# First-batch scores from h^T and S h^T in a two-layer graph kernel: score path, weight loads and epilogue order changed

## The chip, the cores and the metric

The kernel runs on one core of a Trainium2 chip. The metric is the device time of one execution in microseconds (us). The core has a matrix engine (TensorE, PE in the profile; its weight loads are listed apart as PEld), a vector engine (VectorE, DVE), a scalar engine (ScalarE, ACT), a general engine (GpSimd, POOL) and a queue engine for transfers (SyncE, SP). Each engine works through its own instructions in the order in which the program lists them for it; between engines, semaphores carry "this is ready".

## The reference, cut to what matters

There are 16 batches of 1024 nodes with 128 features and a symmetric 0/1 adjacency per batch. Layer 0 is a gated attention layer, layer 1 a tanh attention with four heads; both are followed by a residual and a layer norm.

```python
h = x @ Ww.T + Wb
e = (h @ A) @ h.T
e = e + e.T                      # = h S h^T with S = A + A^T
scores = where(adj > 0, e, 0.0)
attention = softmax(scores, axis=1) * adj
h_prime = relu(attention @ h)
ic, fc, oc = sigmoid(h_prime @ wi_u + x @ wi_x), ...
x = layernorm(x + oc * tanh(ic * h_prime + fc * x))
# layer 1, per head: h1 = X conv_w + conv_b
hh = relu(tanh(adj * (h1 attn_w h1^T)) @ h1)
x = layernorm(x + relu(relu(mean over heads) + x))
```

The scores of layer 0 are softmaxed down a column, and e is symmetric, so the kernel treats a row of blocks as the column that it needs.

## The kernel before, in words

A batch's 1024 nodes are eight blocks of 128. In layer 0, `score(j)` (line 343) multiplies block j against the blocks from j on and writes them to `R`; `turn_score(j)` (line 359) turns the blocks beyond the diagonal and writes them to the rows still to come, by PE transposes and ACT copies in the first batch (b = 0), and through DRAM in the others. `find_edges` (line 391) makes a 0/1 mask of the adjacency; `mask(j)` (line 401) multiplies row j by it on DVE while taking the row's maximum, and ACT takes the exponential with its sum. `weigh(j)` (line 414) divides h by that sum (`hz`), multiplies the row by the adjacency on DVE, and starts `back(j - 1)` (line 431), which adds the previous row's share of the output on PE.

Scores come from a fused form: e_jk = x_j (W^T S W) x_k^T + a part that depends on j alone + a part that depends on k alone. `q_w` is W^T S W, `c_col` is added as the q projection's bias (`project_q`, line 306), and the part by row, r, is made as one more column of `multiply_h` (line 323); `add_h` (line 333) adds it a bias. The eviction of a score (line 353) adds r from column G - 1 of `h`, so it waits for `h`. The first rows of h have to be made before the first score leaves PSUM.

The chain of the fused weights is written at lines 142 to 166: A and Ww are loaded and turned, then S W, q_w, c_col and S b. Six idle matmuls (`keep_at_work`) stand ahead of it and one in its midst. `join_weights` (line 168) is a generator in three parts for layer 1: a difference of convolution weights, its transposes, its product with the attention weights, and another product `ms`; each part ends with an ACT copy of 128x512.

`load_late_weights` (line 99) issues the late loads on SP: three gate columns, a convolution bias, `cw_last` to partitions 1 to 127, `cw_in` in two parts, `aw`, and `wu_b`. On SP's queue they stand behind the first batch's eight adjacency loads, `x` and the second batch's xT, and ahead of the second's adjacency.

The order of the work at the start is written out by hand, as names of pieces that `run` (line 577) calls: W xT, L adjacency, X x, Q the q projection, H and h the product and sum for h, S scores, T turns, A mask with exponential, E edges, B weigh, R ReLU, P rows of h', G gates, I inner gate with tanh, O outer gate, V and N the layer norm. `first` and `second` are batches 0 and 1; the second's pieces stand among the first's to give PE work. After that, `layer1_step` (line 613) runs over 16 batches, four heads and eight blocks, with the coming batches' pieces in tables (`BETWEEN`, `AHEAD`, `FIRST`). Small PSUM tiles share four buffers (`small`, line 61), so a fifth waits for the first's eviction.

The end of the first batch's layer 0 is a chain: the ReLU (line 440), `rows_hp` (line 446), `gates` and `forget` (line 483), `inner` (line 519), `outer` (line 531) and `turn_first_x1` (line 588), which makes x1^T for layer 1; `head_uT` and `rows` then start layer 1.

Of the kernel before, what the change touches and what calls it, by code (L numbers as in the profile page):

```python
# [19 lines left out]
P = 128  # L20
# [4 lines left out]
def two_layer_adjacency_kernel(  # L25
# [19 lines left out]
    nc = tc.nc  # L45
# [15 lines left out]
    def small(name):  # L61
        return ps_sc.tile([P, 512], F32, tag="sc", name=name)
# [7 lines left out]
    nc.gpsimd.memset(mhalf, -0.5)  # L70

    a_in = sb.tile([P, P], F32, tag="hz", name="a_in", bufs=4)
    nc.scalar.dma_start(a_in, A)
    ww_in = sb.tile([P, P], F32, tag="hz", name="ww_in", bufs=4)
    nc.sync.dma_start(ww_in, Ww)
    wb_col = consts.tile([P, 1], F32, name="wb_col")
    nc.scalar.dma_start(wb_col, Wb.rearrange("(d o) -> d o", o=1))
    rows_x = sb.tile([3, P], F32, tag="s1", name="rows_x", bufs=4)
# [18 lines left out]
    wu_b = consts.tile([P, 3, D], F32, name="wu_b")  # L97

    def load_late_weights():
        for g, w in enumerate((wi_u, wf_u, wo_u)):  # L100
            nc.sync.dma_start(gate_u[:, g : g + 1], w.rearrange("(d o) -> d o", o=1))
        nc.sync.dma_start(cw_in[0:1], conv_b.rearrange("(o h) d -> o h d", o=1))
        nc.sync.dma_start(cw_last[1:P], conv_w[:, D - 1, :].partition_broadcast(P - 1))
        for f0, f1 in ((0, 112), (112, D - 1)):
            nc.sync.dma_start(
                cw_in[1 + f0 : 1 + f1], conv_w[:, f0:f1, :].rearrange("h f d -> f h d")
            )
        nc.sync.dma_start(aw, attn_w.rearrange("h i j -> i h j"))
        for g, w in enumerate((wi_u, wf_u, wo_u)):
            nc.sync.dma_start(wu_b[:, g, :], w.partition_broadcast(P))  # L110


# [5 lines left out]
    nc.gpsimd.memset(cw_last[0:1], 0.0)  # L118
# [23 lines left out]
    pa, pw, ps, pc = small("p_a"), small("p_ww"), small("p_s"), small("p_c")  # L142
    nc.tensor.transpose(pa[:, :P], a_in, ident)
    nc.vector.tensor_add(a_sym, pa[:, :P], a_in)
    nc.tensor.matmul(pw[:, :P], ww_in, ident, start=True, stop=True)
    nc.scalar.copy(wwT, pw[:, :P])
    nc.gpsimd.tensor_copy(b_wide, wb_col.to_broadcast([P, P]))
    nc.tensor.matmul(ps[:, :P], a_sym, ww_in, start=True, stop=True)
    nc.vector.tensor_copy(s_ww, ps[:, :P])
    keep_at_work(1)  # L150
    pq, px = small("p_q"), small("p_x")
    nc.tensor.matmul(pq[:, :P], s_ww, ww_in, start=True, stop=True)
    nc.vector.tensor_copy(q_w, pq[:, :P])
    nc.tensor.matmul(pc[:, 0:1], s_ww, wb_col, start=True, stop=True)
    nc.vector.tensor_copy(c_col, pc[:, 0:1])
    nc.tensor.matmul(pc[:, 1:2], a_sym, wb_col, start=True, stop=True)
    nc.vector.tensor_copy(sb_col, pc[:, 1:2])

    def gates_x():
        nc.tensor.matmul(px[:, :3], rows_x, ident[:3, :3], start=True, stop=True)  # L160
        nc.vector.tensor_copy(gate_x, px[:, :3])

    def finish_weights():
        pt = small("p_bsb")
# [2 lines left out]

    def join_weights():

        nc.vector.tensor_sub(cw, cw_in, cw_last)  # L170
        pt = small("p_cwT")
        for hd in range(H):
            nc.tensor.transpose(pt[:, ts(hd, P)], cw[:, hd, :], ident)
        nc.scalar.copy(cwT.rearrange("p h f -> p (h f)"), pt)
# [4 lines left out]
        nc.scalar.copy(caT.rearrange("p h f -> p (h f)"), pt)  # L179
# [103 lines left out]
    def layer0(b):  # L283
# [22 lines left out]
        def project_q(q):  # L306
            if q == 0:
                t["qT"] = sb.tile([P, N], F32, tag="qT0", name=f"qT0_{b}", bufs=1)
            if (b, q) == (0, 1):
                ps = small("pT_q0_second")  # L310
                nc.tensor.matmul(ps, q_w, t["xT"][:, 512:], start=True, stop=True)
                nc.vector.tensor_scalar_add(t["qT"][:, 512:], ps, c_col)
                return
            if (b, q) != (0, 0):
                return project_T(t["qT"], q_w, t["xT"], c_col, f"q0_{b}", [q])
            ps = small("pT_q0_first")
            nc.tensor.matmul(ps, q_w, t["xT"][:, :512], start=True, stop=True)
            for at, to in ((0, P), (P, 512)):
                nc.scalar.activation(
                    t["qT"][:, at:to], ps[:, at:to], AF.Identity, bias=c_col  # L320
                )

        def multiply_h(g):

# [8 lines left out]
        def add_h(g):  # L333
            h, ks = t["h"], GROUPS[g]
            nc.vector.tensor_add(
                h[:, ks[0] : ks[-1] + 1, :], t["ph", g],
                wb_row.unsqueeze(1).to_broadcast([P, len(ks), G]),
            )
            if g == len(GROUPS) - 1:
                t["gate"] = sb.tile([P, NB, 3], F32, tag="gate", name=f"gate_{b}")  # L340
                nc.vector.tensor_copy(t["gate"], h[:, :, D : D + 3])

        def score(j, halves=None):
            if j == 0:
# [53 lines left out]
            engine.tensor_scalar(m, adj_t[b, j], 0.0, None, ALU.is_gt)  # L398
            t["edge", j] = m.rearrange("p (k d) -> p k d", d=P)

        def mask(j):
            s, nmax = t["R"][:, :, j, :], -3e38
            for ks in (ts(0, BH), ts(1, BH)) if (b, j) == (0, 0) else [slice(NB)]:
                top = sb.tile([P, 1], F32, tag="top", name=f"top_{b}_{j}_{ks.start}", bufs=4)
                nc.vector.tensor_tensor_reduce(  # L405
                    s[:, ks], s[:, ks], t["edge", j][:, ks], 1.0, nmax, ALU.mult, ALU.max, top
                )
                nmax = top
            nmax = sb.tile([P, 1], F32, tag="nmax", name=f"nmax_{b}_{j}", bufs=4)
            nc.vector.tensor_scalar_mul(nmax, top, -1.0)  # L410
            t["z", j] = sb.tile([P, 1], F32, tag="z", name=f"z_{b}_{j}", bufs=4)
            nc.scalar.activation(s, s, AF.Exp, bias=nmax, accum_out=t["z", j])  # L412

        def weigh(j):

# [155 lines left out]
            if j + 1 < NB:  # L571
                pieces[f"T{j}"] = partial(turn_score, j)
        if b == 0:
            del pieces["S1"], pieces["T0"]
        return pieces

    def run(pieces, names):
# [297 lines left out]
```

## Time and profile before

The median is 2413.15 us of 3 runs (2412.75 to 2415.81). The profiled execution took 2412.88 us, with a span of 2410.9 us on the core and a granted TensorE clock of 0.999.

| what | value |
|---|---|
| PE busy | 2399.1 us (100% of the span) |
| DVE busy | 1554.7 us (64%) |
| ACT busy | 1065.3 us (44%) |
| POOL busy | 603.3 us (25%) |
| DMA, mean | 82 GB/s |

Busy time is the time in which an engine has an instruction in work; a PE that is busy is not one at its peak, since matmuls overlap each other. The chain that ended last is followed back from the last instruction, at each step to what released it. A float32 matmul shows as two records with two weight loads; a transpose shows as one.

### The profile page before, as it was taken

The numbers are of one execution on the slowest core, as the hardware profiler recorded it, in microseconds if no ns is written. First come the engines' busy times: TensorE is split into PE (matmuls) and PEld (weight loads), VectorE is DVE, ScalarE is ACT, GpSimd is POOL, SyncE is SP. The second block draws the span as 40 slices with busy tenths as digits, with TensorE's granted clock in tenths as the row PEclk, the third lists the DMA queues.
The fourth block names the chain that finished last, engine by engine and source line by source line (L and its number), as shares of the span: only waits on it lengthen the run. The fifth ranks groups of instructions, "written<-read, shape, count | busy, mean of one in ns | idle before, by whom it ended". The sixth has DMA issues, their size and how long they took to land.

```text
span 2410.9 us, 20160 instructions
## 1 busy us (share of the span) xinstructions
PE 2399.1 (100%) x5981; PEld 1095.2 (45%) x5981; DVE 1554.7 (64%) x3280; ACT 1065.3 (44%) x1500; POOL 603.3 (25%) x373
## 2 busy tenths in 40 slices
PE   8999999999999999999999999999999999999999
PEld 5444444444444444444444444444444444444444
DVE  7666666666667666676666665666666576666555
ACT  6544344443444444445344454434444344443333
POOL 1314131241312413123131231312214132141000
PEclk9999999999999999999999999999999999999999
DMA  5334151341514424243242422425234252341010
GB/s 185 79 75 126 36 139 36 95 115 48 127 44 100 101 52 123 50 108 87 60 115 57 113 75 70 105 61 123 61 72 112 53 127 57 79 114 34 18 27 9
DMA packets 474349, 197.04 MB, mean 82 GB/s; under 512 B 414964, under 2 KB 440303, under 8 KB 474240
## 3 DMA queue, kind: packets, MB, share of 16 engines
q1 hardware_dynamic: 455626, 129.03, 22.9%
q0 software_dynamic: 18320, 66.66, 9.4%
q8 instruction: 48, 0.79, 0.1%
q14 instruction: 61, 0.50, 0.1%
q10 hardware_dynamic: 294, 0.07, 0.0%
HBM read 136.19 MB, written 59.51 MB: 81 GB/s over the span
## 4 chain that ended last, share of the span: by engine, by line
PE 98%; DVE 1%; ACT 0%; issue 0%; POOL 0%; POOLq 0%; DVEq 0%; ACTq 0%
PE sc L630 36%; PE acc L636 36%; PE acc L435 9%; PE sc L350 5%; PE pR L601 5%; PE pT_u L234 5%; PE pR_h L331 1%; PE pT_q L234 1%; DVE R L405 0%; DVE R L427 0%; PE idle L139 0%; DVE st L210 0%; DVE edge L398 0%; DVE u L523 0%; PE pt L454 0%
## 5 line engine op out<-in xcount | busy, mean ns | idle before, releaser
L631 DVE TENSOR_TENSOR s<-sc,adj 128x512 f32<-128x512 f32 x1008 | 685.5, 688 | 711.8 <-PE sc L630 688.3
L632 ACT ACTIVATE s<-s 128x1024 f32<-128x1024 f32 x504 | 533.9, 1059 | 1055.9 <-DVE s L631 896.6
L630 PE MATMUL sc<-uT,x1T 128*128 128x512 f32 x2048 | 962.4, 592 | 0.0
L636 PE MATMUL acc<-s,h 128*128 128x512 f32 x2016 | 947.3, 592 | 0.0
L636 PEld LDWEIGHTS acc<-s,h 128*128 128x128 f32 x2016 | 380.5, 190 | 484.7 <-issue 477.5
L630 PEld LDWEIGHTS sc<-uT,x1T 128*128 128x128 f32 x2048 | 386.9, 190 | 469.3 <-issue 403.5
L398 POOL TENSOR_SCALAR edge<-adj 128x1024 uint8<-128x1024 f32 x120 | 332.8, 2773 | 316.2 <-DVE top_None L405 314.1
L214 POOL TENSOR_TENSOR rs<-rs,mhalf 128x8 f32<-128x8 f32 (+3 forms) x35 | 54.0, 1543 | 884.4 <-DVE rs L213 884.4
L435 PE MATMUL acc<-R,hz 128*128 128x512 f32 x512 | 240.8, 593 | 2.3 <-DVE R L427 1.4
L412 ACT ACTIVATE R<-R,nmax 128x1024 f32<-128x1024 f32 x128 | 147.3, 1151 | 84.9 <-DVE nmax L410 76.0
L405 DVE CUSTOM_DVE_ANT_0 R<-R,edge 128x1024 f32<-128x1024 f32 (+1 forms) x128 | 154.9, 1210 | 0.5 <-PE turn L368 0.5
L427 DVE TENSOR_TENSOR R<-R,adj 128x1024 f32<-128x1024 f32 x129 | 154.6, 1199 | 0.0
L435 PEld LDWEIGHTS acc<-R,hz 128*128 128x128 f32 x512 | 96.6, 190 | 124.7 <-issue 115.0
L350 PE MATMUL sc<-xT,qT 128*128 128x512 f32 (+3 forms) x384 | 145.2, 487 | 0.5 <-ACT R L369 0.3
L353 ACT ACTIVATE R<-sc,h 128x512 f32<-128x512 f32 (+1 forms) x192 | 111.1, 581 | 51.6 <-PE sc L350 44.1
L467 POOL TENSOR_TENSOR x1T<-hp,wu_b 128x1024 f32<-128x1024 f32 x45 | 106.4, 2363 | 103.2 <-DVE hws L473 63.7
L234 PE MATMUL pT_u<-x1T,ms 128*128 128x512 f32 x256 | 120.5, 592 | 0.0
L601 PE MATMUL pR<-cw,x1T 128*128 128x512 f32 x256 | 117.7, 598 | 0.0
L350 PEld LDWEIGHTS sc<-xT,qT 128*128 128x128 f32 x384 | 69.6, 190 | 69.6 <-issue 59.8
L300 POOL DMA_DIRECT2D adj<-in_adjT_dram x112 | 65.7, 587 | 92.6 <-DVE s L631 92.6
L654 DVE SCALAR_TENSOR_TENSOR sum<-acc,sum 128x512 f32<-128x512 f32 x95 | 61.3, 686 | 42.2 <-PE acc L636 42.2
L604 ACT COPY h<-pR 128x512 f32<-128x512 f32 x128 | 72.5, 593 | 27.9 <-PE pR L601 26.1
(144 smaller groups left out, 1129.3 us busy)
## 6 DMA issues: line engine op xcount, KB each, us to landing
adj<-in_adjT_dram POOLq DMA_DIRECT2D x112, 512.0 KB, 4.0
adj<-in_adjT_dram SPq DMA_DIRECT2D x16, 512.0 KB, 8.4
x<-in_x_dram SPq DMA_DIRECT2D x16, 512.0 KB, 5.3
xT<-in_xT_dram SPq DMA_DIRECT2D x15, 512.0 KB, 4.6
dram_hp<-turn_hp SPq DMA_DIRECT2D x15, 512.0 KB, 2.6
hp<-dram_hp SPq DMA_DIRECT2D x60, 128.0 KB, 3.2
dram_x<-turn_x SPq DMA_DIRECT2D x15, 512.0 KB, 2.9
x1T<-dram_x SPq DMA_DIRECT2D x60, 128.0 KB, 5.4
```

Of the source, the lines that this page charges most:

```text
L234: nc.tensor.matmul(ps, w, src[:, ts(q, 512)], start=True, stop=True)
L350: nc.tensor.matmul(ps[:, : at - lo], t["qT"][:, ts(j, P)], t["xT"][:, lo:at], start=True, stop=True)
L398: engine.tensor_scalar(m, adj_t[b, j], 0.0, None, ALU.is_gt)
L405: nc.vector.tensor_tensor_reduce(s[:, ks], s[:, ks], t["edge", j][:, ks], 1.0, nmax, ALU.mult, ALU.max, top)
L412: nc.scalar.activation(s, s, AF.Exp, bias=nmax, accum_out=t["z", j])
L427: nc.vector.tensor_mul(s[:, ks], s[:, ks], adj[:, ks])
L435: nc.tensor.matmul(t["acc"][:, ts(q, 512)], t["hz", j], t["R"][:, ts(q, BH), j, :], start=(j == 0), stop=(j == NB - 1),)
L601: nc.tensor.matmul(ps, x1T_t[b][:, ts(k, P)], cw.rearrange("p h d -> p (h d)"), start=True, stop=True)
L630: nc.tensor.matmul(ps, x1T[:, ts(m, P)], uT[:, ts(q, 512)], start=True, stop=True)
L631: nc.vector.tensor_mul(s[:, ts(q, 512)], ps, adj[:, ts(q, 512)])
L632: nc.scalar.activation(s, s, AF.Tanh)
L636: nc.tensor.matmul(acc[:, ts(q, 512)], h1[:, ts(hd, D)], s[:, ts(q, 512)], start=(m == 0), stop=(m == NB - 1),)
```

## The change

For the first batch the scores are taken from h^T itself. `project_h` makes h^T from Ww^T and xT (pieces K0 and K1; `place_h`, k1, is the second half's eviction), and `project_g` makes S h^T in three parts (g0 to g2 of 128, 384 and 512 columns), evicted on DVE. A score is then a product of S h^T and h^T, and its eviction is a plain copy without the row's number. The pieces Q0 and Q1 of the first batch go; q_w, c_col, S b and the row number are still made, since the other batches use them, but behind the first scores (`weigh_Ww`, `weigh_all`).

Ww is loaded ahead of A, on ACT's queue instead of SP's, and turned first, by a transpose. The first row's mask, its exponential and its score are cut into pieces of their own (A0.0, A0.1, A0.e, S0.0, S0.1). Late weights are loaded ahead of x and of the second batch's xT, and `cw_last` is loaded to all 128 partitions, with row 0 set to zero after that. The subtraction in `join_weights`, and the copy of the gates' columns in `add_h` (in every batch), go from DVE to POOL. The generator of joined weights has one stop more, and its parts stand among the rows of the first batch, instead of in the epilogue. In the epilogue the second batch's scores S0 to S4 and Q1 stand in another order; H2 and h2 follow later. `hz` of row 5 of the first batch goes from ACT to DVE.

```diff
-    nc.sync.dma_start(ww_in, Ww)
+    nc.scalar.dma_start(ww_in, Ww)
     nc.scalar.dma_start(a_in, A)
...
-        for g, w in enumerate((wi_u, wf_u, wo_u)):
-            nc.sync.dma_start(gate_u[:, g : g + 1], w.rearrange("(d o) -> d o", o=1))
-        nc.sync.dma_start(cw_last[1:P], conv_w[:, D - 1, :].partition_broadcast(P - 1))
+        nc.sync.dma_start(cw_last, conv_w[:, D - 1, :].partition_broadcast(P))
...
+            nc.sync.dma_start(gate_u[:, g : g + 1], w.rearrange("(d o) -> d o", o=1))
             nc.sync.dma_start(wu_b[:, g, :], w.partition_broadcast(P))
...
+    nc.tensor.transpose(pw[:, :P], ww_in, ident)
+    nc.scalar.copy(wwT, pw[:, :P])
+    keep_at_work(1)
     nc.tensor.transpose(pa[:, :P], a_in, ident)
     nc.vector.tensor_add(a_sym, pa[:, :P], a_in)
-    nc.tensor.matmul(pw[:, :P], ww_in, ident, start=True, stop=True)
...
+    def weigh_Ww():
+        ps = small("p_s")
+        nc.tensor.matmul(ps[:, :P], a_sym, ww_in, start=True, stop=True)
+        nc.vector.tensor_copy(s_ww, ps[:, :P])
+    def weigh_all():
+        pq, px = small("p_q"), small("p_x")
+        nc.tensor.matmul(pq[:, :P], s_ww, ww_in, start=True, stop=True)
+        nc.tensor.matmul(px[:, 4:5], s_ww, wb_col, start=True, stop=True)
+        nc.tensor.matmul(px[:, :3], rows_x, ident[:3, :3], start=True, stop=True)
+        nc.tensor.matmul(px[:, 3:4], a_sym, wb_col, start=True, stop=True)
+        nc.vector.tensor_copy(q_w, pq[:, :P])
+        nc.vector.tensor_copy(c_col, px[:, 4:5])
+        nc.vector.tensor_copy(gate_x, px[:, :3])
+        nc.vector.tensor_copy(sb_col, px[:, 3:4])
...
-        nc.vector.tensor_sub(cw, cw_in, cw_last)
+        nc.gpsimd.memset(cw_last[0:1], 0.0)
+        nc.gpsimd.tensor_sub(cw, cw_in, cw_last)
+        yield
...
+        def project_h(q):
+            ps = small(f"p_hT_{q}")
+            nc.tensor.matmul(ps, wwT, t["xT"][:, ts(q, 512)], start=True, stop=True)
+            if q:
+                t["p_hT"] = ps
+                return
+            for at, to in ((0, P), (P, 512)):
+                nc.scalar.activation(hT[:, at:to], ps[:, at:to], AF.Identity, bias=wb_col)
+        def place_h():
+            nc.vector.tensor_scalar_add(t["hT"][:, 512:], t["p_hT"], wb_col)
+        def project_g(at, to):
+            ps = small(f"p_g_{at}")[:, : to - at]
+            nc.tensor.matmul(ps, a_sym, t["hT"][:, at:to], start=True, stop=True)
+            nc.vector.tensor_copy(t["qT"][:, at:to], ps)
...
-                nc.vector.tensor_copy(t["gate"], h[:, :, D : D + 3])
+                nc.gpsimd.tensor_copy(t["gate"], h[:, :, D : D + 3])
...
-                    ps[:, : at - lo], t["qT"][:, ts(j, P)], t["xT"][:, lo:at], start=True, stop=True
+                    ps[:, : at - lo], t["qT"][:, ts(j, P)], t["xT" if b else "hT"][:, lo:at],
+                    start=True, stop=True,
                 )
+                if b == 0:
+                    nc.scalar.copy(
+                        t["R"][:, lo // P : at // P, j, :],
+                        ps[:, : at - lo].rearrange("p (k d) -> p k d", d=P),
+                    )
+                    continue
...
-            if b == 0 and j in (0, 1, NB - 2, NB - 1):
+            if b == 0 and j in (0, 1, NB - 3, NB - 2, NB - 1):
...
-    run(first, "W L0 L1 L2 L3 L4 L5 L6 L7 X")
-    run(second, "W")
-    load_late_weights()
-    run(second, "L0 L1 L2 L3 L4 L5 L6 L7")
-    run(first, "Q0")
-    gates_x()
-    finish_weights()
-    run(first, "E0 H0 h0 E1 E2 S0 T0.0 S1.0 T0.1 S1.1 A0 E3 T1 S2 A1 Q1 E4 H1 h1 B0 T2 S3 A2 E5 B1")
-    run(first, "H2 h2 T3 S4 A3 E6 B2")
-    run(first, "T4 S5 A4 E7 B3 T5 S6 A5 B4 T6 S7 A6")
+    run(first, "W L0 L1 L2 L3 L4 L5 L6 L7")
+    load_late_weights()
+    run(first, "X")
+    run(second, "W")
+    run(second, "L0 L1 L2 L3 L4 L5 L6 L7")
+    run(first, "K0 K1 g0 k1")
+    weigh_Ww()
+    run(first, "S0.0 S0.1 E0 T0.0 A0.0 g1 T0.1 A0.1")
+    weigh_all()
+    run(first, "S1.0 S1.1 A0.e E1 H0")
+    finish_weights()
+    run(first, "h0 T1 S2 A1 E2 g2 H1 h1 B0 E3 T2 S3 A2 E4 B1")
+    next(join)
+    run(first, "H2 h2 T3 S4 A3 E5")
+    next(join)
+    run(first, "B2 T4 S5 A4 E6")
+    next(join)
+    run(first, "B3 T5 S6 A5 E7")
+    next(join, None)
+    run(first, "B4 T6 S7 A6")
...
     run(second, "h1")
-    next(join)
     run(first, "G")
-    run(second, "S0")
-    next(join)
+    run(second, "S0.0")
     run(first, "I0")
-    run(second, "H2 S1")
+    run(second, "S0.1")
     run(first, "I1")
-    next(join, None)
-    run(second, "h2 S2")
+    run(second, "S1 Q1 S2")
     run(first, "O0 V0 O1")
-    run(second, "S3")
+    run(second, "S3 S4")
     run(first, "N0")
     turn_first_x1(x1_t[0], 0)
-    run(second, "Q1")
-    run(first, "V1 N1")
+    run(second, "H2")
+    run(first, "V1")
+    run(second, "h2")
+    run(first, "N1")
```

More of the change, by code (lines that the diff above doesn't have):

```diff
@@ L72, in two_layer_adjacency_kernel @@
     a_in = sb.tile([P, P], F32, tag="hz", name="a_in", bufs=4)
+    ww_in = sb.tile([P, P], F32, tag="hz", name="ww_in", bufs=4)
+    nc.scalar.dma_start(ww_in, Ww)
     nc.scalar.dma_start(a_in, A)
-    ww_in = sb.tile([P, P], F32, tag="hz", name="ww_in", bufs=4)
-    nc.sync.dma_start(ww_in, Ww)
     wb_col = consts.tile([P, 1], F32, name="wb_col")
@@ L117, in two_layer_adjacency_kernel @@
     cw_last = sb.tile([P, H, D], F32, tag="s1", name="cw_last", bufs=4)
-    nc.gpsimd.memset(cw_last[0:1], 0.0)
     aw = sb.tile([P, H, D], F32, tag="s1", name="aw", bufs=4)
@@ L141, in two_layer_adjacency_kernel @@
     keep_at_work(6)
-    pa, pw, ps, pc = small("p_a"), small("p_ww"), small("p_s"), small("p_c")
+    pa, pw = small("p_a"), small("p_ww")
+    nc.tensor.transpose(pw[:, :P], ww_in, ident)
+    nc.scalar.copy(wwT, pw[:, :P])
+    keep_at_work(1)
     nc.tensor.transpose(pa[:, :P], a_in, ident)
     nc.vector.tensor_add(a_sym, pa[:, :P], a_in)
-    nc.tensor.matmul(pw[:, :P], ww_in, ident, start=True, stop=True)
-    nc.scalar.copy(wwT, pw[:, :P])
     nc.gpsimd.tensor_copy(b_wide, wb_col.to_broadcast([P, P]))
[L148 to L159, printed above, removed]
+    def weigh_Ww():
[6 more added lines that the diff above has]
+        nc.tensor.matmul(px[:, 4:5], s_ww, wb_col, start=True, stop=True)
         nc.tensor.matmul(px[:, :3], rows_x, ident[:3, :3], start=True, stop=True)
+        nc.tensor.matmul(px[:, 3:4], a_sym, wb_col, start=True, stop=True)
+        nc.vector.tensor_copy(q_w, pq[:, :P])
+        nc.vector.tensor_copy(c_col, px[:, 4:5])
         nc.vector.tensor_copy(gate_x, px[:, :3])
+        nc.vector.tensor_copy(sb_col, px[:, 3:4])
     def finish_weights():
@@ L308, in project_q @@
                 t["qT"] = sb.tile([P, N], F32, tag="qT0", name=f"qT0_{b}", bufs=1)
[L309 to L312, printed above, removed]
+            project_T(t["qT"], q_w, t["xT"], c_col, f"q0_{b}", [q])
+        def project_h(q):
+            if q == 0:
+                t["hT"] = sb.tile([P, N], F32, tag="turn", name="hT", bufs=2)
+            hT, at = t["hT"], q * 512
+            ps = small(f"p_hT_{q}")
+            nc.tensor.matmul(ps, wwT, t["xT"][:, ts(q, 512)], start=True, stop=True)
+            if q:
+                t["p_hT"] = ps
                 return
[L314 to L317, printed above, removed]
             for at, to in ((0, P), (P, 512)):
-                nc.scalar.activation(
-                    t["qT"][:, at:to], ps[:, at:to], AF.Identity, bias=c_col
-                )
+                nc.scalar.activation(hT[:, at:to], ps[:, at:to], AF.Identity, bias=wb_col)
+        def place_h():
+            nc.vector.tensor_scalar_add(t["hT"][:, 512:], t["p_hT"], wb_col)
+        def project_g(at, to):
+            if at == 0:
+                t["qT"] = sb.tile([P, N], F32, tag="qT0", name=f"qT0_{b}", bufs=1)
+            ps = small(f"p_g_{at}")[:, : to - at]
+            nc.tensor.matmul(ps, a_sym, t["hT"][:, at:to], start=True, stop=True)
+            nc.vector.tensor_copy(t["qT"][:, at:to], ps)
         def multiply_h(g):
@@ L340, in add_h @@
                 t["gate"] = sb.tile([P, NB, 3], F32, tag="gate", name=f"gate_{b}")
-                nc.vector.tensor_copy(t["gate"], h[:, :, D : D + 3])
+                nc.gpsimd.tensor_copy(t["gate"], h[:, :, D : D + 3])
         def score(j, halves=None):
-            if j == 0:
+            if j == 0 and "R" not in t:
                 t["R"] = sb.tile([P, NB, NB, P], F32, tag="R", name=f"R_{b}", bufs=1)
@@ L399, in find_edges, with mask, exponentials @@
             t["edge", j] = m.rearrange("p (k d) -> p k d", d=P)
[L401 to L404, printed above, removed]
+        def mask(j, halves=None):
+            s, nmax = t["R"][:, :, j, :], t.get("top", -3e38)
+            for ks in [slice(NB)] if halves is None else [ts(q, BH) for q in halves]:
+                t["top"] = sb.tile([P, 1], F32, tag="top", name=f"top_{b}_{j}_{ks}", bufs=4)
                 nc.vector.tensor_tensor_reduce(
-                    s[:, ks], s[:, ks], t["edge", j][:, ks], 1.0, nmax, ALU.mult, ALU.max, top
+                    s[:, ks], s[:, ks], t["edge", j][:, ks], 1.0, nmax, ALU.mult, ALU.max, t["top"]
                 )
-                nmax = top
-            nmax = sb.tile([P, 1], F32, tag="nmax", name=f"nmax_{b}_{j}", bufs=4)
-            nc.vector.tensor_scalar_mul(nmax, top, -1.0)
+            if halves != [0]:
+                t["nmax", j] = sb.tile([P, 1], F32, tag="nmax", name=f"nmax_{b}_{j}", bufs=4)
+                nc.vector.tensor_scalar_mul(t["nmax", j], t.pop("top"), -1.0)
+            if halves is None:
+                exponentials(j)
+        def exponentials(j):
+            s = t["R"][:, :, j, :]
             t["z", j] = sb.tile([P, 1], F32, tag="z", name=f"z_{b}_{j}", bufs=4)
-            nc.scalar.activation(s, s, AF.Exp, bias=nmax, accum_out=t["z", j])
+            nc.scalar.activation(s, s, AF.Exp, bias=t["nmax", j], accum_out=t["z", j])
         def weigh(j):
@@ L573, in layer0 @@
         if b == 0:
-            del pieces["S1"], pieces["T0"]
+            del pieces["S1"], pieces["T0"], pieces["A0"], pieces["Q0"], pieces["Q1"]
+            for q in range(NH):
+                pieces[f"K{q}"] = partial(project_h, q)
+                pieces[f"A0.{q}"] = partial(mask, 0, [q])
+            for g, (at, to) in enumerate(((0, P), (P, 512), (512, N))):
+                pieces[f"g{g}"] = partial(project_g, at, to)
+            pieces["k1"] = place_h
+            pieces["A0.e"] = partial(exponentials, 0)
+        if b <= 1:
+            del pieces["S0"]
+            for q in range(NH):
+                pieces[f"S0.{q}"] = partial(score, 0, [q])
         return pieces
```

## The prediction, made before the changed kernel was run

> **What bounds the kernel now.** I read the page first: busy shares, then the chain that ended last.
>
> ```profile
> PE 2399.1 (100%) x5981; PEld 1095.2 (45%) x5981; DVE 1554.7 (64%) x3280; ACT 1065.3 (44%) x1500; POOL 603.3 (25%) x373
> ...
> PE 98%; DVE 1%; ACT 0%; issue 0%; POOL 0%; POOLq 0%; DVEq 0%; ACTq 0%
> ```
>
> TensorE (PE) carries 98% of the chain; what the change touches can pay only where PE has room. That is the start, so next I took busy time by stage (columns: stretch, length, busy us of PE, PEld, DVE, ACT, POOL with instruction counts, PE clock, DMA share, GB/s).
>
> ```profile
> 9.56:15.64 6.08, 4.98 (x23) 2.80 (x22) 4.68 (x10) 4.35 (x7) 0.00 (x0) 1.00 1.02 415
> 15.64:39.25 23.61, 20.94 (x75) 10.62 (x73) 22.60 (x47) 17.31 (x37) 0.00 (x0) 1.00 0.56 147
> 39.25:43.04 3.79, 3.79 (x11) 1.82 (x11) 2.04 (x5) 0.00 (x0) 0.00 (x0) 1.00 1.03 418
> 43.04:56.98 13.94, 13.10 (x69) 8.74 (x68) 11.01 (x47) 11.20 (x24) 1.89 (x3) 1.00 0.32 126
> 21.00:30.00 9.00, 8.06 (x27) 4.11 (x28) 8.83 (x20) 5.55 (x11) 0.00 (x0) 1.00 0.08 22
> ```
>
> The reader sees three regimes. From 15.64 to 39.25 VectorE (DVE) works 22.60 of 23.61 us: it sets the pace of the eight attention rows. From 39.25 PE finishes row sums. From 43.04 to 56.98 runs the epilogue, a chain of small steps; from 57 on PE has 5.00 of every 5 us. The last line shows that the DMA engines idle meanwhile at 0.08. How each stage begins is in the timeline (start, us, engine, line, operation):
>
> ```profile
> 9.56 0.69 DVE L398 TENSOR_SCALAR edge<-adj 128x1024 bf16<-128x1024 f32 x1 [0.93 <-DMA adj<-in_adjT_dram]
> ...
> 12.71 0.69 DVE L405 CUSTOM_DVE_ANT_0 R<-R,edge 128x512 f32<-128x512 f32 x1
> 15.64 1.23 DVE L405 CUSTOM_DVE_ANT_0 R<-R,edge 128x1024 f32<-128x1024 f32 x1 [0.52 <-PE turn L368]
> 17.69 0.75 DVE L312 TENSOR_SCALAR qT<-pT_q_second,wwT_g 128x512 f32<-128x512 f32 x1 [0.62 <-PE pT_q_second L311]
> ...
> 17.21 0.24 SPq L103 DMA_DIRECT2D cw_last<-in_L_gnn_conv_w_dram  x1
> 18.55 12.28 SPq L105 DMA_DIRECT2D cw_in<-in_L_gnn_conv_w_dram  x2
> ...
> 46.22 0.59 ACT L174 COPY cwT<-p_cwT 128x512 f32<-128x512 f32 x1
> 49.85 0.57 ACT L179 COPY caT<-p_caT 128x512 f32<-128x512 f32 x1
> 50.31 0.64 ACT L527 ACTIVATE u<-u 128x512 f32<-128x512 f32 x1
> 56.15 0.59 ACT L594 COPY x1T<-pt 128x512 f32<-128x512 f32 x1 [0.97 <-PE pt L593]
> ```
>
> The first edge mask waits for the adjacency load until 9.56; the first row's mask (L405) starts only at 12.71, the second row's at 15.64. The weight load for the joined weights holds SP's queue for 12.28 us. In the epilogue two ACT copies of joined weights stand before the tanh at 50.31.
>
> **What the skill says.** "Trace analysis" (Perfetto Trace Analysis, Identifying the Most-Contended Engine): PE busy share is not closeness to its peak. It agrees: counting PE records at the 0.43 us that one 128x512 record takes in the row sums (the chain has four score records of L630 in 1.72 us), 15.64 to 39.25 holds 19.9 us of work where 20.94 is busy. So PE has some 3.7 us free there, and 1.6 us of 13.9 in the epilogue.
> "DMA: Bandwidth & Descriptors" (Why a DMA increments its semaphore by 16 and not by 1): 127 partitions put a whole transfer on one of 16 engines, 128 on all. Before, `cw_last` fills 127 partitions, and the stretch 21 to 30 shows 0.08 of 16 engines: it agrees.
> "SBUF — State Buffer" (SBUF: two separate sides): GpSimd and some DVE operations exclude each other. The trace agrees in part: one tensor_scalar of L225 took 1061 ns (median 345) beside a POOL edge at 58.07, while L427 never exceeded 1220.
>
> **The change part by part.** PE's total work first. K0, K1 replace Q0, Q1; g0 to g2 (128+384+512 columns) are extra: 4 records of 0.43 = +1.72 us of PE. The transpose for Ww instead of a two-record matmul gives back about 0.2. Everything else on PE only moves.
>
> *Start.* Ww is transposed first (3.97, when the six idle matmuls end) and copied by ACT after its table load. Estimate: ww_in and xT are issued at about 0.7 from different queues; a_in and wb_col move back one ACT issue (0.45), to land near 3.4 and 5.0. The table load now ends about 4.5 (it ended 4.05), copy 0.27, K0 at 4.85 + 1.0, first h^T piece 6.3, all 512 at 6.8 (0.84 for the two). K1 and g0 end near 7.1, g0's DVE copy 7.4, first score 7.5 to 8.4 (before: 9.15). Row bias and h are no longer needed. Copy 0.59: half a row at 9.0.
>
> *First row.* E0 still waits for the adjacency, which I leave at 9.56: its issue was behind wb_col and a_in, and removing ww_in from SP is offset by these landing later. E0 0.62, so the mask's first half starts at 10.25, against 12.71. Then on DVE g1's copy (0.50), second half (0.75 with readout and nmax 0.95), and the copies of q_w, c_col, gate_x, sb_col (0.29 + 3 x 0.15, pitch about 0.6): to 13.05. E1 to 13.67. Meanwhile PE: T0.1 ends about 10.75, four small weight matmuls with loads 1.1, S1 1.5, ACT copy to 14.0, T1 0.66: second row's mask at about 15.0, against 15.64. DVE idles some 0.5 before it.
>
> *Rows.* I sum DVE, since it paces. Before, from 9.56 to the product of row 6 (ends 39.25): 29.69 us, of which 27.28 busy. Added pitches: g1 0.50, weight copies 0.6, p_bsb (came earlier before) 0.1, row 5's hz now on DVE (NB - 3) 0.2; g2 0.68 takes the place of Q1's 0.68; gate copy leaves, -0.1. Sum +1.3. Idle before 2.4 (adjacency 1.5, L312 0.6, rest), now about 1.1 (0.5 above, 0.3 for g2, 0.3 rest). Row 6 ends where it was: 39.25 + 1.3 - 1.3. The 2.4 us gained at the first mask are thus eaten by work moved behind it.
> Then joined weights: 0.43 + 0.86 + 0.86 = 2.15 us of PE and three ACT copies of 0.59 enter rows 3 to 5. PE's row 4 becomes 1.72 (sum) + 0.33 (turn) + 0.65 (score) + 0.95 (joined, with load bubbles) = 3.65, while DVE's row takes 1.26 + 0.60 + 1.26 = 3.12. PE starts with slack, since each sum runs one row behind; over rows 3 to 5 it loses about 0.4 a row. Bounds 0 and 1.5; I take +0.5 for row 6.
> The subtraction for cw goes to POOL. Not shown there; between POOL's 0.71 (128x256 product) and 2.36 (128x1024): 1.2. It runs as soon as weights land. Its lock could stretch one edge by up to 1.2 (bound 0 to 1.2, in the 0.5). SP's queue: late weights before x and second xT. Eight adjacency loads end near 18.5 (the first at 9.56, then 1.28 us each as between the waits at 10.82 and 12.10); 0.96 MB at 415 GB/s are 2.3 us, landing about 21 to 22, cw ready about 23.5. PE reaches p_cwT near 24.5. x (wanted at 47), second xT (wanted at 33.5) and the second adjacency (wanted at 58) land by about 24, 25 and 36. Behind POOL's wait stand only the gate copies, wanted at the next gates. These edits cost nothing, hidden there.
>
> *Epilogue.* Same row sums, so ReLU at 43.04 + 0.5. Removed: 2.15 us PE filler, which doesn't carry the chain. gate exp no longer stands behind cwT: 46.70 to 46.41, -0.29. The tanh L527 had waited behind two score copies and caT; h2 and gate (0.55) stood ahead of O0. Now inner products end at 50.15, O0 starts there, against 51.01: -0.86. ACT afterwards has S1, Q1, S2, S3, S4: tanh ends 51.0, then 1.16 + 0.65 + 1.06 + 0.95 + 0.65 = 4.5, so the copy of x1T goes at 55.5 rather than 55.25, when its transposes are ready. It was 56.15. u_T thus starts about 56.14 instead of 56.98: -0.84. PE's rest is smaller by S4 (0.86), done ahead, while H2 (0.45) fits in front of u_T as Q1 (0.86) did.
>
> *Sum* from this execution: +0.5 - 0.84 - 0.86 = -1.2, so 2410.9 becomes 2409.7. Later batches: the gate copy (178 ns on DVE) on POOL, which has 25%; PE does not wait for it: 0. Against the median 2413.15 (runs to 2415.81; the profiled one's 2412.88) I forecast 2412.0. 0.2% is 4.8 us, about what a measurement of this kernel can tell from no change.
>
> **Rivals.**
> A, faster beyond the sum: the 2.4 us at the first mask are kept because DVE's old idle time absorbs added work, and PE keeps up. -2.4 - 1.7 = -4.1, 2409. For: L312's wait and both adjacency waits go. Against: DVE's added 1.3.
> B, slower: cw late. PE takes instructions in order; if p_cwT waits for POOL, all sums, turns and thereby DVE wait. Before, the second cw_in was issued at 30.03 and landed 4.7 later. If one-engine behaviour persisted, with issue some 5 earlier, cw would stand at about 31; beyond 24.5 plus 0.5 slack each us costs one: +6.5 - 1.2, about 2418.5. It decides from about 31 on. Against: wu_b, broadcast to 128, landed in 4.7 to 6.2 us.
> C, no help: rows become PE- and ACT-paced. ACT per row: exp 1.2, hz 0.39, turn 0.5, score 0.6, joined 0.59 = 3.3 against DVE's 3.12, PE 3.65: row 6 two to three us later, +2.5 - 1.7 = +1, with the epilogue delayed too up to +3: 2414 to 2416.
>
> **How the numbers follow.** My forecast 0.55, C 0.27, A 0.10, B 0.08. A reaches over 0.2% in about four of ten, B in most, C hardly: faster 0.04, same 0.88, slower 0.08. The likeliest's own range is 2410.5 to 2413.5; taking in C's 2416 and half of A, 2409.2 to 2416.0 leaves out under 2 in 10.
>
> **What would show it.** Right: first L405 near 10.3, second near 15, row 6's L427 ending 39 to 40, no L170 subtraction on DVE, cw loads landed by 23, x1T's first copy near 56, PE without gaps after it. Wrong: an idle PE before p_cwT in rows, DVE waiting for turns by over 2 us, adjacency landing much off 9.5, or evictions S3, S4 standing before x1T's copy for over a us.

## The result and the profile after

The changed kernel takes 2418.18 us (median of 22 runs, 2416.74 to 2420.18), the kernel before 2412.99 us in the same comparison (22 runs, 2412.6 to 2415.87). The ratio is 1.0018, with a 95% interval of 1.0012 to 1.0025: it is slower, by 5.2 us from median to median. Six of the 22 executions of the kernel before lie near 2415.8 and the others near 2412.8, so the means differ by less, 4.4 us, which is what the ratio says. The forecast was 2412.0 with a range up to 2416.0, so the time lies outside it, on the side of the slow rivals. The profiled execution has a span of 2415.5 us, 4.6 more than before.

First the page's busy line and the chain that ended last, of the changed kernel:

```profile
PE 2403.2 (99%) x5986; PEld 1096.3 (45%) x5986; DVE 1553.9 (64%) x3267; ACT 1061.7 (44%) x1499; POOL 608.7 (25%) x390
...
PE 96%; DMA 1%; DVE 1%; SPq 0%; ACT 0%; issue 0%; POOL 0%; ACTq 0%; POOLq 0%; DVEq 0%
```

PE's busy time rose by 4.1 us. By the prediction's count 1.7 of that is all the work that was added; another 1.6 lies in K0 and K1, whose records took 1.06 us each where they take 0.59 with Ww on SP's queue (an experiment below). The new entry is "DMA 1%": the chain now begins with transfers, the bias `wb_col` first. Then the four stages of the prediction, with the same columns:

```profile
9.56:15.64 6.08, 4.60 (x23) 2.98 (x23) 3.17 (x8) 2.84 (x6) 0.29 (x1) 1.00 0.91 349
15.64:39.25 23.61, 21.88 (x102) 13.67 (x102) 21.68 (x47) 16.09 (x35) 2.92 (x3) 1.00 0.86 289
39.25:43.04 3.79, 3.79 (x14) 2.00 (x13) 3.72 (x8) 2.31 (x6) 0.00 (x0) 1.00 0.13 52
43.04:56.98 13.94, 12.52 (x45) 6.28 (x43) 9.18 (x30) 7.88 (x18) 0.75 (x2) 1.00 0.00 0
```

DVE's 3.17 us in the first stage, against 4.68 before, say that it starts late; its 3.72 of 3.79 in the third say that the rows, which had ended there, are still running. The timeline shows how late (start, us, engine, line):

```profile
1.62 10.43 SPq L303 DMA_DIRECT2D adj<-in_adjT_dram  x8
1.64 0.45 ACTq L77 DMA_DIRECT2D wb_col<-in_L_gnn_Wb_dram  x1
10.37 0.84 ACT L325 ACTIVATE hT<-p_hT,wb_col 128x128 f32<-128x128 f32 x2 [4.70 <-DMA wb_col<-in_L_gnn_Wb_dram]
12.38 0.68 DVE L419 TENSOR_SCALAR edge<-adj 128x1024 bf16<-128x1024 f32 x1
14.22 0.69 DVE L426 CUSTOM_DVE_ANT_0 R<-R,edge 128x512 f32<-128x512 f32 x1 [1.16 <-PE turn L406]
19.39 1.23 DVE L426 CUSTOM_DVE_ANT_0 R<-R,edge 128x1024 f32<-128x1024 f32 x1
...
43.60 1.22 DVE L453 TENSOR_TENSOR R<-R,adj 128x1024 f32<-128x1024 f32 x1
...
60.88 0.59 ACT L631 COPY x1T<-pt 128x512 f32<-128x512 f32 x1
```

The loss is there before the first row begins. To write the first piece of h^T, ACT needs p_hT, the product of K0, and `wb_col`, the bias of 512 bytes. It stands still for 4.70 us. K0 is done at about 7.8; the bias, issued at 1.64, lands only at about 10.3. Everything in order behind it shifts: g0, the copy that DVE makes of it, and on DVE the first edge mask, which stands behind that copy (12.38, though its adjacency would have let it start before). The first row's mask starts 1.5 us later than in the kernel before instead of 2.5 earlier, as predicted; the second's starts at 19.39 instead of 15.64.

The milestones below hold the kernel before, the prediction and the changed kernel against each other. The last column is an experiment told next (the changed kernel with Ww on SP's queue); us from the span's start.

| step | before | predicted | after | Ww on SP |
|---|---|---|---|---|
| bias landed (its first use on POOL) | 4.6 | 5.0 | 10.3 | 5.1 |
| first row's mask starts | 12.71 | 10.25 | 14.22 | 10.39 |
| second row's mask starts | 15.64 | 15.0 | 19.39 | 15.52 |
| product of row 6 ends | 39.25 | 39.75 | 44.82 | 41.32 |
| u_T's first matmul | 56.81 | 56.47 | 61.52 | 58.02 |
| span | 2410.9 | 2409.7 | 2415.5 | 2411.9 |

The prediction's own figure for u_T is 56.14, but that leaves out the 0.5 us by which it had the rows end later, and it counts from 56.98, the chain's time for this matmul, which the timeline shows at 56.81. The table has both put right: 39.75 + 17.56 - 0.84 = 56.47.

### The profile page after: what moved, and what is told of

Same layout as the page of the kernel before. It is cut to its first block, busy times and chain, and to the rows that moved or that the text cites. A ratio compares the mean times of both kernels' runs of the same rounds, so it can differ in the third digit from the quotient of the medians.

```text
span 2415.5 us, 20176 instructions
## 1 busy us (share of the span) xinstructions
PE 2403.2 (99%) x5986; PEld 1096.3 (45%) x5986; DVE 1553.9 (64%) x3267; ACT 1061.7 (44%) x1499; POOL 608.7 (25%) x390
## 4 chain that ended last, share of the span: by engine, by line
PE 96%; DMA 1%; DVE 1%; SPq 0%; ACT 0%; issue 0%; POOL 0%; ACTq 0%; POOLq 0%; DVEq 0%
PE sc L667 36%; PE acc L673 36%; PE acc L461 9%; PE sc L364 5%; PE pT_u L237 4%; PE pR L638 4%; PE pR_h L345 1%; PE pT_q L237 1%; DMA adj<-in_adjT_dram 1%; DMA wb_col<-in_L_gnn_Wb_dram 0%; DMA aw<-in_L_gnn_attn_w_dram 0%; DVE R L426 0%; DVE R L453 0%; DVE st L213 0%; DMA R<-dram_turn 0%; SPq L267 0%
## 5 line engine op out<-in xcount | busy, mean ns | idle before, releaser
L364 PE MATMUL sc<-xT,qT 128*128 128x512 f32 (+2 forms) x360 | 135.7, 487 | 0.6 <-ACT R L374 0.6
L374 ACT ACTIVATE R<-sc,h 128x512 f32<-128x512 f32 (+2 forms) x180 | 103.9, 579 | 48.6 <-PE sc L364 43.4
```

Of the source, the lines that this page charges most:

```text
L364: nc.tensor.matmul(ps[:, : at - lo], t["qT"][:, ts(j, P)], t["xT" if b else "hT"][:, lo:at], start=True, stop=True,)
```

## The experiments

Two theories stood against each other. W: the loss is the late bias, because the adjacency loads now get ahead of it. D: the loss is the work added on DVE and PE ahead of and among the rows. Medians are given with their comparison to the kernel before, which took 2412.89 to 2412.99 in the three sets.

**The bias first on ACT's queue**

```diff
+    nc.scalar.dma_start(wb_col, Wb.rearrange("(d o) -> d o", o=1))
     nc.scalar.dma_start(ww_in, Ww)
     nc.scalar.dma_start(a_in, A)
-    nc.scalar.dma_start(wb_col, Wb.rearrange("(d o) -> d o", o=1))
```

> The changed kernel with one line moved: wb_col is the first load on ACT's queue, ahead of Ww and A. Theory W (the loss is the late bias: wb_col landed at 10.3 because its small packets, issued at 1.64, fell behind the adjacency loads that now start at 1.62): it lands near 4, the first h^T piece is written near 7 instead of 10.4, and the time falls by about 4 us, to 2413 to 2414. Rival D (the loss is the DVE and PE work added ahead of the rows and the joined weights among the rows): the bias is early but the last row ends within 1 us of where it does in the changed kernel, 2417 to 2418.

2416.81 us (18 runs), ratio 1.0014 (1.0007 to 1.0021): my expectation of 2413 to 2414 missed. POOL used the bias at 4.4, as W says, but now the other loads were late. The waits of PE (engine, tile, line, what ended it: us, times, longest):

```profile
PE p_ww L141 <- DMA ww_in<-in_L_gnn_Ww_dram: 1.6, 1, 1.6
PE p_a L144 <- DMA a_in<-in_L_gnn_A_dram: 0.5, 1, 0.5
```

PE works in order, so K0 behind A's transpose (6.94) starts at 7.21, where the prediction had 4.85. A second cost comes on top: the four records of K0 and K1 take 3.62 us, where the next run has 2.23 (1.06 us a record instead of 0.59); why they are longer is not shown. The first row's mask starts at 14.42, as late as in the changed kernel. Which load is the victim changed, the loss remained; D could still be true by this run alone.

**Ww on SP's queue again, ahead of xT**

```diff
-    nc.scalar.dma_start(ww_in, Ww)
+    nc.sync.dma_start(ww_in, Ww)
     nc.scalar.dma_start(a_in, A)
```

> The changed kernel with Ww's load put back on SP's queue, ahead of xT; the bias is second on ACT's queue again and the adjacency loads start later, as in the kernel before. Theory W: wb_col lands between 4.5 and 5.5, time 2413 to 2414. Rival D: no change, 2417 to 2418.

2413.54 us (12 runs), ratio 1.0001 (0.9993 to 1.0010): the loss is gone but for some 0.6 us that lie within the interval. The adjacency issues begin at 2.83 again, and the bias lands in time. The masks then stand where the prediction had them:

```profile
10.39 0.69 DVE L426 CUSTOM_DVE_ANT_0 R<-R,edge 128x512 f32<-128x512 f32 x1 [0.18 <-PE turn L406]
15.52 1.23 DVE L426 CUSTOM_DVE_ANT_0 R<-R,edge 128x1024 f32<-128x1024 f32 x1
20.29 0.99 DVE L419 TENSOR_SCALAR edge<-adj 128x1024 bf16<-128x1024 f32 x1
21.32 2.21 POOL L172 TENSOR_TENSOR cw<-cw_in,cw_last 128x512 f32<-128x512 f32 x1 [0.60 <-DMA cw_in<-in_L_gnn_conv_w_dram]
22.52 1.57 DVE L419 TENSOR_SCALAR edge<-adj 128x1024 bf16<-128x1024 f32 x1
```

All of D's added work is in this kernel, so D falls as the cause of the 5.2 us. The last three lines show a smaller cost: beside POOL's work on the joined weights two edge masks of 0.68 us take 0.99 and 1.57.

**The gate rows on SP, between xT and the adjacency**

```diff
-    for g, w in enumerate((wi_x, wf_x, wo_x)):
-        nc.scalar.dma_start(rows_x[g : g + 1], w.rearrange("(o d) -> o d", o=1))
...
-    run(first, "W L0 L1 L2 L3 L4 L5 L6 L7")
+    run(first, "W")
+    for g, w in enumerate((wi_x, wf_x, wo_x)):
+        nc.sync.dma_start(rows_x[g : g + 1], w.rearrange("(o d) -> o d", o=1))
+    run(first, "L0 L1 L2 L3 L4 L5 L6 L7")
```

> The changed kernel with the three gate rows loaded by SP, between xT and the adjacency, instead of by ACT; Ww, A and the bias stay in their order on ACT's queue. The adjacency loads start about 1.2 us later, at about 2.9, and ACT's table load no longer stands behind the sixth issue. Theory W in its narrow form (the adjacency loads overtake the bias): wb_col, still third and issued at 1.64, lands near 5 and the time is 2412.5 to 2414. If the place on ACT's queue is what delays it (third behind two 64 KB loads), it lands at 9 to 10 still, and the time stays at 2417 or a little below, for the earlier table load. Rival D: 2417 to 2418 whatever the landing.

2413.83 us (12 runs), ratio 1.0003 (0.9994 to 1.0011). Here Ww, A and the bias keep their places on ACT's queue and the bias is issued at 1.64 as in the changed kernel; the adjacency starts later, at 3.81 (2.9 was expected). ACT's table load moves ahead too, so it is the landing of the bias that decides here, more than the time. The adjacency's issues and the time from issue to landing of `wb_col`, of this kernel:

```profile
3.81 3.76 SPq L301 DMA_DIRECT2D adj<-in_adjT_dram  x8
...
DMA to landing us min/median/max: 3.3/3.3/3.3
```

In the changed kernel the last line says 8.6. So the third place on ACT's queue is not enough to delay the bias: what decides is when the adjacency starts.

One rival was not varied: POOL's own load of the same bias, broadcast to 128 partitions (`wb_row`), which POOL issues at 1.60 in every one of these kernels. Its packets go by queue q0, those of ACT's loads by q10 (packets, MB, share of the 16 DMA engines in one microsecond). The changed kernel from 5 to 6 us and from 9 to 10, then the kernel before from 4 to 5:

```profile
q0 software_dynamic: 13, 0.05, 148.2%
q10 hardware_dynamic: 72, 0.00, 3.9%
...
q10 hardware_dynamic: 11, 0.00, 0.6%
...
q0 software_dynamic: 12, 0.05, 153.7%
q10 hardware_dynamic: 2, 0.00, 0.1%
```

In the changed kernel ACT's small packets are still in work when POOL's come, and the last 24 follow between 8 and 10 us; in the kernel before they were nearly through by then (2 packets). With the adjacency at 3.81, POOL's packets from 4 to 5 us show 22.0%. So the early adjacency may have delayed the bias only into POOL's load, and that load may have done the rest. No run moves `wb_row`, so how the delay divides between the two is not shown; that the start of the adjacency decides is.

**That one line alone, in the kernel before**

```diff
-    nc.scalar.dma_start(a_in, A)
-    nc.sync.dma_start(ww_in, Ww)
+    nc.scalar.dma_start(ww_in, Ww)
+    nc.scalar.dma_start(a_in, A)
```

> The kernel before with one part of the change alone: Ww is loaded on ACT's queue ahead of A, so the bias becomes third and the adjacency loads start about a microsecond earlier. Theory W: the bias lands late here too (8 to 10); the fused weights' bias c_col waits for it and with it the first q, so the first row starts some 2 to 4 us later, and the time is 2415 to 2417. Rival D: the loads have nothing to do with it, 2412.5 to 2413.5.

2420.71 us (6 runs), ratio 1.0030 (1.0018 to 1.0043), more than expected: 7.8 us above the kernel before, from moving one load of 64 KB to another queue and ahead of A. PE's longest wait in that stage, of this kernel:

```profile
PE p_c L154 <- DMA wb_col<-in_L_gnn_Wb_dram: 2.5, 1, 2.5
```

The bias landed 8.4 us after its issue, and the first row's mask started at 19.00 instead of 12.71. That is more than the wait alone: the product for c_col, p_c, starts 4.3 us later than in the kernel before (10.11 against 5.85), the first score 6.65 later (15.80 against 9.15), since PE's records in between are longer here as well (those of the first q, 128x512, 1.06 us and more, where the kernel before has 0.59 to 0.68). The load order alone makes the loss, with nothing of the new scores.

**The subtraction on VectorE** (with Ww on SP's queue, as in all that follow)

```diff
-        nc.gpsimd.memset(cw_last[0:1], 0.0)
-        nc.gpsimd.tensor_sub(cw, cw_in, cw_last)
+        nc.scalar.mul(cw_last[0:1], cw_last[0:1], 0.0)
+        nc.vector.tensor_sub(cw, cw_in, cw_last)
```

> The changed kernel with Ww on SP's queue again (the early bias), and in addition the subtraction for the joined weights on VectorE, with row 0 set to zero by ScalarE, at the same place among the rows; nothing of it on POOL. If POOL's lock costs VectorE time (two edge masks of 684 ns took 0.99 and 1.57 us beside POOL's zeroing and subtraction with Ww on SP), all eight edges take 0.68 to 0.70, the subtraction adds 0.68, and the last rows end 0.5 us earlier: about 0.4 below the kernel with Ww on SP, 2413.1. If the edges were long for another reason, they stay long and the time rises by 0.7, to 2414.2.

2413.65 us, ratio 1.0004 (0.9995 to 1.0012), so no gain in time. All eight edges take 0.68 to 0.69, which shows that POOL's work was what stretched them (0.3 + 0.9 = 1.2 us). But the subtraction costs DVE 0.68, and PE's transposes wait 1.0 us for it. Row 6's product ends at 41.39, as with Ww on SP alone (41.32). The second row's mask had started 0.66 us later in this execution, though (16.18), ahead of anything that this change touches. Counted from there, the rows took 25.2 us, against 25.3 to 25.8 in the five executions that have POOL's subtraction among the same rows: 0.1 to 0.6 us less, where 0.5 was expected, and not clear of the spread.

**The joined weights in the epilogue, first trial**, on top of the zeroing on ScalarE and the subtraction on VectorE

```diff
-    next(join)                       # and three more among the rows
+    next(join)                       # zeroing, subtraction and turns, behind "h1"
+    next(join)
     run(first, "G")
     run(second, "S0.0")
+    next(join)
     run(first, "I0")
     run(second, "S0.1")
     run(first, "I1")
+    next(join, None)
```

> As the kernel with Ww on SP's queue, with the joined weights back in the epilogue: all their parts stand where the kernel before had them, and the subtraction is on VectorE. If they cost the rows only POOL's lock (1.2 us) and filled PE's free time otherwise, the rows end 1.2 us earlier, near 40.1 for the product of row 6, while the epilogue gets 0.3 to 0.9 longer: 2413.0 to 2413.5. If they made PE pace the rows, as the second slow rival says, the rows end 2 us or more earlier, and the time is 2412 or less.

2416.70 us (20 runs), ratio 1.0014 (1.0007 to 1.0021). Row 6's product ended at 39.62, 1.7 us earlier than with Ww on SP, but the zeroing stood on ACT behind the ReLU, so the subtraction on DVE waited 2.4 us with the gate chain behind it. The trial tells the price in the rows and nothing of the epilogue: from the second row's mask (15.28) the rows took 24.3 us, against the 25.3 to 25.8 above, so 0.9 to 1.5 us less.

**cw_last to 127 partitions, as before the change**

```diff
-        nc.sync.dma_start(cw_last, conv_w[:, D - 1, :].partition_broadcast(P))
+        nc.sync.dma_start(cw_last[1:P], conv_w[:, D - 1, :].partition_broadcast(P - 1))
```

> As the kernel with Ww on SP's queue, with cw_last loaded to partitions 1 to 127 as before, row 0 zeroed at the start. This makes rival B of the prediction real: the load goes to one of the 16 DMA engines, cw is ready near 30 rather than near 23.5, PE waits some 6 us before the transposes of cw, and the time is 2418 to 2421. If the number of partitions doesn't matter, 2413.5 as with Ww on SP.

2422.54 us (4 runs), ratio 1.0039 (1.0024 to 1.0054). PE's longest wait:

```profile
PE p_cwT L176 <- POOL cw L172: 8.6, 1, 8.6
```

POOL's subtraction could only start at 31.48, where it starts at 21.32 with Ww on SP. Rival B is a real mechanism. Its price, 9.0 us above the kernel with Ww on SP, is more than the 6.5 it was given and lies above the expectation; the changed kernel avoids it through the 128th partition.

**Less on VectorE**

```diff
-            nc.vector.tensor_copy(t["qT"][:, at:to], ps)
+            (nc.scalar.copy if at == 512 else nc.vector.tensor_copy)(t["qT"][:, at:to], ps)
-        nc.vector.tensor_copy(q_w, pq[:, :P])
+        nc.scalar.copy(q_w, pq[:, :P])
...                                    # E2 from behind A1 to ahead of finish_weights()
```

> As the kernel with Ww on SP's queue, with less on VectorE ahead of and among the rows: the copies of q_w and of the last 512 columns of S h^T go to ScalarE, and the third edge mask stands before the wait for the bias of the row number instead of behind the second row's mask. If VectorE paces the rows, each of these shows in full: 0.3 + 0.7 + 0.6 us, the product of row 6 ends near 39.7 instead of 41.3, and the time is 2411.9 to 2412.3. If PE or ScalarE paces them, the time stays within 0.5 us of 2413.5.

2413.39 us, ratio 1.0001 (0.9992 to 1.0010). Row 6's product ends at 40.69, 0.6 us earlier where 1.6 were expected, and half of that (0.34) was there at the second row's mask. DVE's waits for h, of the kernel with Ww on SP and then of this one:

```profile
DVE h L349 <- PE pR_h L345: 2.4, 1, 2.4
```

```profile
DVE h L349 <- PE pR_h L345: 3.7, 2, 2.4
```

The second kernel has one wait more, of 1.3 us: with DVE relieved it stands before h1 until PE has done S2, g2 and H1. There PE sets the pace, not DVE. From the second row's mask the rows took 25.5 us, no less than before.

**The joined weights in the epilogue, second trial**

```diff
         nc.gpsimd.memset(cw_last[0:1], 0.0)
-        nc.gpsimd.tensor_sub(cw, cw_in, cw_last)
         yield
+        nc.vector.tensor_sub(cw, cw_in, cw_last)
...                                    # parts stand as in the first trial
```

> As the kernel with Ww on SP's queue, with the joined weights in the epilogue: only the zeroing of row 0 stays on POOL among the rows, the subtraction is on VectorE behind the second batch's second sum, where the kernel before had it, and nothing of it waits on ScalarE's zeroing any more (that was what stretched the first trial of this). Price of the joined weights among the rows, read from the first trial: 1.7 us of row time. If the epilogue needs less than that for them, the product of row 6 ends near 39.8, u_T starts 17.2 to 17.7 later, near 57.3, and the time is 2412.6 to 2413.2. If the epilogue gives all of it back, 2413.5 or more.

2413.81 us, ratio 1.0001 (0.9992 to 1.0010). Row 6's product ends at 39.81, 1.5 us before the kernel with Ww on SP. u_T starts at 58.45, which is 18.6 later, against 16.7. The epilogue takes 1.9 us more, and gives all of it back: PE waits 1.0 us for the ACT copy of caT (the second part of the joined weights) alone. The place among the rows is no loss on balance, and no gain that shows.

**S4 back in layer 1's first steps**

```diff
-    run(second, "S3 S4")
+    run(second, "S3")
```

> As the kernel with Ww on SP's queue, with the score S4 of the second batch back among the first steps of layer 1. The prediction took 0.86 us off for S4 made ahead. If VectorE paces those first steps, PE only waits where S4 stood, and the time stays at 2413.5, with 0.2 us either way; if the 0.86 us was real, the time rises to 2414.4, less what the epilogue saves.

2414.28 us, ratio 1.0006 (0.9997 to 1.0014), higher than expected. In its profiled execution the second mask started 0.65 later (16.17 against 15.52), ahead of anything that this change touches, so the total does not decide. From u_T's first matmul to the span's end it does: 2354.1 us here (2412.5 - 58.39), 2353.9 with S4 ahead (2411.9 - 58.02), 2354.1 in the kernel before. S4 made ahead spares some 0.2, not 0.86. Even the 0.2 is not clear: the nine other executions with S4 ahead lie between 2353.6 and 2354.4. The PE weight loads' waits show why, of the kernel with S4 ahead and of the one with S4 back:

```profile
PEld sc L667 <- DVE s L668: 1.8, 2, 0.9
```

```profile
PEld sc L667 <- DVE s L668: 0.6, 2, 0.4
```

Without S4 between them, the scores of layer 1 wait 1.2 us longer for DVE's evictions.

**Edges of rows 4 to 7 on POOL**, on top of "less on VectorE"

```diff
-            engine = nc.gpsimd if b else nc.vector
+            engine = nc.gpsimd if b or j >= 4 else nc.vector
...                                    # E5 moved to behind E4
```

> As the kernel with less on VectorE, with the edge masks of rows 4 to 7 of the first batch on POOL (2.77 us each in the other batches) instead of VectorE. If VectorE's work paces the rows, 2.5 us less of it bring the product of row 6 to 38.5 to 39.5 instead of 40.7, PE becoming the pace, and the time to 2411 to 2412.3, below both kernels. If POOL's lock stretches VectorE's small operations as much as it saves, or PE paces the rows already, 2413.0 to 2414.

2412.70 us, ratio 0.9998 (0.9989 to 1.0006): the fastest of all, 5.5 us below the changed kernel, and not to be told from the kernel before. Row 6's product ends at 40.55, only 0.14 us earlier than with less on VectorE, although four edges of about 0.6 left DVE; the second row's mask had started 0.46 later (15.64 against 15.18). The DVE and POOL timelines of this kernel:

```profile
26.31 5.87 POOL L419 TENSOR_SCALAR edge<-adj 128x1024 bf16<-128x1024 f32 x2
...
26.45 1.97 DVE L453 TENSOR_TENSOR R<-R,adj 128x1024 f32<-128x1024 f32 x1
29.74 1.79 DVE L453 TENSOR_TENSOR R<-R,adj 128x1024 f32<-128x1024 f32 x1
```

These two products take 0.6 and 0.75 us more than their 1.2, beside a POOL edge. A third, at 19.28, ran beside one too (18.01 to 20.77) and took 1.22. Together with the second row's mask (1.71 instead of 1.23) and one hz (0.91 instead of 0.29) the loss is 2.4 us, of the 2.4 to 2.5 moved. The kernel it is compared with had lost 0.9 on one edge (1.57) in the same way, so from the second mask the rows are 0.6 us shorter (24.9 against 25.5).

## Why the prediction was wrong, point by point

**The start is the step that failed.** The prediction had a_in and wb_col "land near 3.4 and 5.0" and left the adjacency "at 9.56", since "removing ww_in from SP is offset by these landing later". It counted the shift of ACT's issues (0.45 us), and not what SP would then do: its first adjacency load went from 2.91 to 1.62, beside the bias instead of behind it. The bias took 8.65 us instead of 3.4. The first h^T piece was priced at 6.3 and came at 10.74 (10.37 plus 0.37). The profile before held the warning (the adjacency's issues on SP's queue, and that queue's waits for loads of ACT's):

```profile
2.91 5.44 SPq L300 DMA_DIRECT2D adj<-in_adjT_dram  x8
...
SPq L300 <- DMA wb_col<-in_L_gnn_Wb_dram: 0.8, 1, 0.8
SPq L300 <- DMA a_in<-in_L_gnn_A_dram: 0.8, 1, 0.8
```

xT's issues end at 2.06; the first adjacency load goes at 2.91, when a_in has landed, and the third at 4.57, when wb_col has. I read these waits as idle and not as protection. That an early adjacency makes the bias late is shown by four runs: with the adjacency from 1.62 or 1.63 on, the bias is late in both kernels; with it from 2.83 (the bias second on ACT's queue) or 3.81 (the bias third), it is in time. Whether its packets then stood behind the adjacency's or behind those of POOL's broadcast is not shown.

A smaller miss lies under it: the table load ended at 5.40 for the 4.5 of the prediction, since ACT's sixth issue waited until 3.86, and K0 started at 5.73 for 4.85. The late bias hid it.

**The first row without that was right.** With Ww on SP, which keeps the adjacency where the prediction left it, masks started at 10.39 and 15.52, for 10.25 and 15.0. The gain of 2.3 us at the first mask is eaten before the second, as the sum said: g1's and the weights' copies, and a wait of 1.3 us for p_bsb (the bias of the row number) where 0.5 was put.

**The rows were 1.6 us too short.** Row 6 was put at 39.75; Ww on SP gave 41.32. Of that, 0.5 us was there when the second mask started. The rest is one mis-sized term, the joined weights among the rows. Without them the sum holds: 24.3 us from the second mask in both trials with them in the epilogue, for 24.25 in the prediction. With them it is 25.3 to 25.8, so they cost 0.9 to 1.5 us where 0.5 was put. What stretched DVE beside POOL is 1.2 us with Ww on SP; the text had given that bounds of 0 to 1.2, and then let it share the 0.5 with PE's pace. How much of it the rows really lost is not clear, since the subtraction on DVE won at most 0.6 back. The Trainium skill's page "SBUF — State Buffer" (SBUF: two separate sides) speaks of an exclusive lock, and these runs agree in part: edges, scalings and two products beside POOL were stretched, a third product was not. My remark that L427 never exceeded 1220 ns holds too: in the kernel before 30 of these products start inside a POOL edge mask of 2.77 us, and none takes over 1.21 us. So a product beside a POOL edge is not always locked out; when it is stays open.

**The epilogue was right, and S4 wrong.** From row 6's product to u_T: 17.56 before, 16.70 after, a gain of 0.86 for the 0.84 forecast. The 0.86 us for S4, subtracted as PE work less, was 0.1 to 0.2 at most: PE is not alone in those first steps. It counted work and did not ask who waits next.

**Rivals.** B, the late cw, was given 2418.5; it did not happen, but the run with 127 partitions shows it. The Trainium skill's page "DMA: Bandwidth & Descriptors" (Why a DMA increments its semaphore by 16 and not by 1) (127 partitions go to one of 16 engines) carried that part rightly: PE waited 8.6 us for that load's user. A slow rival by a late load was the right kind, put on the wrong load. C, the rows paced by PE and ACT, had row 6 end two to three us later and +1 in the sum; with Ww on SP row 6 ends 2.07 later and the span is 1.0 longer. So without the late bias C's numbers come nearer than my forecast's. Its mechanism is shown in part only: relieving DVE did not shorten the rows, but part of what the joined weights cost there is the clash of DVE with POOL, which C does not have. A fell: of the 2.3 us won at the first mask 0.1 was left at the second.

With the terms put right for the kernel with Ww on SP, the sum is +2.07 (row 6) - 0.86 (epilogue) - 0.2 (S4) = +1.0, and its span is 2411.9, +1.0; the terms are read from the same trace, so this only shows that none is missing. For the changed kernel: +5.57 - 0.86 - 0.1 = +4.6, and its span is +4.6.

## What to carry to other kernels

When a load moves to another queue, list what the queue that it left will now issue earlier, and which small transfer that needs to be early then has company: 512 bytes took 8.6 us to land beside bulk. Order urgent small loads so that the bulk behind them is issued only once they are in flight for long enough (1.7 to 2.2 us were enough in these runs), and keep a wait that happens to do this until something else does. A gain on the path counts only as far as the next engine lets it: S4, the edges on POOL and the relieved DVE all moved work away from one engine and met the next wait within a few microseconds.

## What the runs showed of the hardware that was not expected

- A bias of 128 rows of 4 bytes took 3.3 to 3.8 us from issue to landing when the adjacency was issued 1.7 to 2.2 us after it, and 8.4 to 8.6 when it was issued at the same time, on another queue. POOL's broadcast was in flight each time.
- That broadcast of 64 KB, on POOL's queue, shows 138 to 162% of the 16 DMA engines in one microsecond while it moves 0.05 MB, in four kernels; where the adjacency started at 3.81 it shows 22.0%.
- PE's records of 128x512 at the start took 0.59 us in some kernels and 1.06 in others (the changed one, the bias first, and Ww first in the kernel before), with a granted clock of 1.00 in all. The cause is open.
- VectorE beside GpSimd: edge masks of 0.68 us took up to 1.57, scalings of 0.29 up to 1.10, and products of two SBUF inputs, never over 1.22 in the kernel before, up to 1.97.
- A GpSimd subtraction of 128x512 takes 1.26 us, and 2.21 when it meets VectorE; its copy of 128x24 takes 0.20 and 1.13. A clash costs both sides.
- A load to 127 partitions made PE wait 8.6 us for its user; with the same load to 128 PE did not wait there. That was a rival of the prediction; the size was not expected.
